# First cross attention: maxima taken from the SBUF copy of the scores, with turns and values a cycle later

## The chip, the core and the metric

The kernel runs on one core of a Trainium2 chip. The metric is device time in microseconds (us) of one execution, lower is better. Engines are called PE or TensorE (matmul), PEld (its weight load), DVE or VectorE, ACT or ScalarE, POOL or GpSimd, and SP (a queue that issues transfers).

## What is computed

The program is a stack of four layers of attention and feed-forward sections over x (16 x 64 x 256, float32) and a context of 16 x 1601 x 256. The change touches its first section, a cross attention with 16 heads of 16, in which the mask is made of scores that are exactly zero at or below the diagonal:

```python
def _L0_xattn_ref(q, k, v, w_q, w_k, w_v, w_o):
    qp, kp, vp = (_split_head(z) for z in (q @ w_q, k @ w_k, v @ w_v))
    scores = jnp.einsum('bhqd,bhkd->bhqk', qp, kp) / jnp.sqrt(jnp.float32(d_k))
    mask = (scores == PAD) & tril
    scores = jnp.where(mask, neg, scores)
    attn = jax.nn.softmax(scores, axis=-1)
    attn = jnp.where(mask, PAD, attn)
    out = jnp.einsum('bhqk,bhkd->bhqd', attn, vp)
    return concat @ w_o
...
x = x + _L0_xattn_ref(_layernorm(x), ctx_1024, ctx_1024, L0_xattn_w_q, ...)
```

## The kernel before, in words

`l0_xattn` (L223 to L530) works on 32 *units*: a batch element and one half of its heads (8 heads, called g). Keys lie on the partitions, 13 *chunks* of 128 to a unit (the last has 65 real keys). A chunk's scores are four matrices of 128 keys x (two heads x 64 queries), one for each row group r of TensorE. Four chunks make a *tile* of 128 x 2048 float32; it fills four PSUM banks, and there is one such buffer (`sc`, tag w, L343). As 13 is not a multiple of 4, a unit takes 3.25 cycles and most units begin within a tile: over a *round* of 13 cycles the units end in cycles 3, 6, 9 and 12.

The main loop (L492 to L525) does one tile per cycle, q = 0 to 103, and everything in it is kept in program order on each engine (`Written`, `mm`, `tr`; these helpers record ScalarE, VectorE and GpSimd operations at L59 and matmuls at L2739 and L2757). A cycle of before issues, in this order:

- for a unit whose maxima were spread in the cycle before: ScalarE copies `mx` to SBUF (L495)
- `take` (ScalarE copies a finished unit's sums) and, for the tile of four cycles ago, `lower` (L402): GpSimd subtracts `mx` from `raw` in SBUF, one operation for each unit in the tile
- `scores(q)` on TensorE
- exp on ScalarE for tile q - 5
- `hide` (L355), where a unit begins: two VectorE operations on the first chunk in PSUM
- ScalarE copies the tile to SBUF (`raw`, L512; seven buffers from two pools)
- `maxima` (L366): per chunk one VectorE operation, top = max(top, scores in PSUM). In the trace these start when ScalarE's copy of the same tile has ended
- two *pieces* of projection of keys and values for later cycles (L334), into PSUM tag `bk` of two buffers; key pieces are copied out by ScalarE, value pieces by VectorE (`keep_values`), `last_keys` by both. A piece may also start the next context load on SP's queue and a small GpSimd operation (`load`, L269)
- `finish` (four small VectorE operations and a matmul group) between the two pieces, for a unit whose values are complete
- `turn_maxima` (L384) in the cycle where a unit ends: TensorE turns `top` into `mt` (tag `bk`), VectorE reduces it to `m`
- near the end, `out(t)`: output projection of a finished block
- `values(q - 5)` on TensorE, with weights from `v` and the exps as moving data, into `acc`
- `spread_maxima` (L394): TensorE spreads `m` over the partitions into `mx` (tag `bk`)

The constant LAG (5) is the number of cycles between a tile's scores and its values; LEAD (4) sets how far the pieces run ahead. GpSimd's subtraction can begin only when `mx` of its unit is in SBUF.

Of the kernel before, what the change touches and what calls it, by code (L numbers as in the profile page):

```python
# [12 lines left out]
F32 = mybir.dt.float32  # L13
I32 = mybir.dt.int32
BF16 = mybir.dt.bfloat16
AF = mybir.ActivationFunctionType
ALU = mybir.AluOpType
AX = mybir.AxisListType
PSUM = bass.MemoryType.PSUM

P = 128
B, S, D = 16, 64, 256
# [3 lines left out]
SK = 1601  # L26
NCH = 13
# [37 lines left out]
class Sections:  # L65
# [57 lines left out]
    def copy(self, out, in_):  # L123

        self.flip ^= 1
        if self.flip:
            self.nc.vector.tensor_copy(out, in_)
        else:
            self.nc.scalar.copy(out, in_)
# [93 lines left out]
    def l0_xattn(self):  # L223
# [6 lines left out]
        with ExitStack() as ctx:  # L230
            sb = ctx.enter_context(tc.tile_pool(name="l0x", bufs=1, reuse_waits="tile"))
            sb2 = ctx.enter_context(tc.tile_pool(name="l0x2", bufs=2, reuse_waits="tile"))
            ps = ctx.enter_context(tc.tile_pool(name="l0x_ps", bufs=2, space=PSUM, reuse_waits="tile"))
            V, A, G = (Written(tc, e) for e in (nc.vector, nc.scalar, nc.gpsimd))
# [15 lines left out]
            pm = ps.tile([P, 512], F32, tag="acc", name="awake")  # L250
# [8 lines left out]
                [sb2.tile([32, 2, 4 * D], F32, tag="raw", name="bias_raw", bufs=4)[:, i] for i in range(2)],  # L259
                sb2.tile([32, 4 * D], BF16, tag="kT", name="part", bufs=5))  # L260

            UNITS, LAG, LEAD = 2 * B, 5, 4
            Q = UNITS * NCH // 4
            xs, us, raws = {}, {}, {}

# [12 lines left out]
                    own.unsqueeze(1).unsqueeze(3).to_broadcast([P, 2, 2, S]), ALU.mult,  # L278
                )

            def keys(b, g, j):
                x = xs[b]
                pm = ps.tile([P, 512], F32, tag="bk", name="pk")
                for k in range(KC):
                    self.columns(
                        pm, wk[:, k, g * P : (g + 1) * P], x.cT[:, k, 512 * j : 512 * j + 512],
                        start=(k == 0), stop=(k == KC - 1))
                x.kT[g, j] = sb2.tile([P, 512], F32, tag="kT", name="kT", bufs=5)
                A.copy(x.kT[g, j], pm)

            def project_values(x, pm, cs):
                for j, c in enumerate(cs):
                    for k in range(KC):
                        self.columns(
                            pm[:, j * D : (j + 1) * D], x.cT[:, k, c * P : (c + 1) * P], wv[:, k, :],
                            start=(j == 0 and k == 0), stop=(k == KC - 1), skip_group_check=True)

            def keep_values(x, pm, cs):
                V.tensor_copy(
                    x.v[:, cs[0] : cs[0] + len(cs), :, :, :16],  # L300
                    pm[:, : len(cs) * D].rearrange("p (j a h e) -> p j a h e", h=2, e=16, a=H // 2))

            def last_keys(b):
                x = xs[b]
                pm = ps.tile([P, 512], F32, tag="bk", name="pk")
                project_values(x, pm, [NCH - 1])
                for g in range(2):
                    for k in range(KC):
                        self.columns(
                            pm[:, (2 + g) * P : (3 + g) * P], wk[:, k, g * P : (g + 1) * P], x.cT[:, k, 1536:1664],  # L310
                            start=False, stop=(k == KC - 1), skip_group_check=True)
                x.last = sb2.tile([P, 2, P], F32, tag="kl", name="kl")
                A.copy(x.last, pm[:, 256:].rearrange("p (g n) -> p g n", g=2))
                keep_values(x, pm, [NCH - 1])

            def two_values(b, i):
                x = xs[b]
                pm = ps.tile([P, 512], F32, tag="bk", name="pk")
                project_values(x, pm, [2 * i, 2 * i + 1])
                keep_values(x, pm, [2 * i, 2 * i + 1])  # L320

            order = [(keys, 0, 0), "v", (keys, 0, 1), "v", (keys, 0, 2), (last_keys,), "v", (keys, 1, 0), "v",
                     (keys, 1, 1), "v", (keys, 1, 2), "v"]
# [7 lines left out]
                    elif b < B:  # L331
                        pieces.append((p[0], b, *p[1:]))

            def piece(i):  # L334
                if 0 <= i < len(pieces) and pieces[i]:
                    f, *args = pieces[i]
                    f(*args)
                if i % NCH == 4 and 0 < i // NCH + 1 < B:
                    load(i // NCH + 1)

# [14 lines left out]
            def hide(q, pm):  # L355

                for i in range(4):
                    if (4 * q + i) % NCH == 0:
                        shape = [S, 4, P]
                        of = pm[:S, :, i, :]  # L360
                        z = sb2.tile(shape, BF16, tag="z", name="z")
                        V.scalar_tensor_tensor(
                            z, of, 0.0, upto[:S].unsqueeze(1).to_broadcast(shape), ALU.is_equal, ALU.mult)
                        V.scalar_tensor_tensor(of, z, NEVER, of, ALU.mult, ALU.add)

            def maxima(q, pm):  # L366

                for i in range(4):
                    n = 4 * q + i
                    u, c = divmod(n, NCH)  # L370
                    if c == 0:
                        us[u] = Streamed(u)
                        us[u].top = sb2.tile([P, 4, P], F32, tag="top", name="top")
                        V.tensor_copy(us[u].top, pm[:, :, i, :])
                        continue
                    w = min(P, SK - c * P)
                    top = us[u].top[:w]
                    V.tensor_tensor(top, top, pm[:w, :, i, :], ALU.max)

            def ends(q):  # L380

                return [n // NCH for n in range(4 * q, 4 * q + 4) if n % NCH == NCH - 1 and 0 <= n < 4 * Q]

            def turn_maxima(u):  # L384

                pt = ps.tile([P, 4, P], F32, tag="bk", name="mt")
                for r in range(4):
                    for j in range(4):
                        o = slice(32 * j, 32 * j + 32)
                        self.mm(pt[o, r, :], us[u].top[:, r, o], self.ident, start=(r == 0), stop=True, skip_group_check=True)  # L390
                us[u].m = sb2.tile([P, 4], F32, tag="m", name="m")
                V.tensor_reduce(us[u].m, pt, AX.X, ALU.max)

            def spread_maxima(u):  # L394

                pt = ps.tile([P, 4, P], F32, tag="bk", name="mx")
                for r in range(4):
                    self.tr(pt[:, r, :], us[u].m[:, r : r + 1].to_broadcast([P, P]), self.ident)
                us[u].mx = sb2.tile([P, 4, P], F32, tag="mx", name="mx", bufs=3)
                us[u].pt = pt  # L400

            def lower(q, E):  # L402

                n, end = 4 * q, 4 * q + 4
                while n < end:
                    u = n // NCH
                    to = min(end, (u + 1) * NCH)
                    part = raws[q][:, :, n - 4 * q : to - 4 * q, :]
                    E.tensor_tensor(part, part, us[u].mx.unsqueeze(2).to_broadcast([P, 4, to - n, P]), ALU.subtract)
                    n = to  # L410

            def values(q):
                e = raws.pop(q)
# [15 lines left out]
            def take(u):  # L429
                us[u].sums = sb2.tile([P, P], F32, tag="sums", name="sums")  # L430
                A.copy(us[u].sums, us[u].acc[:, :P])
# [58 lines left out]
            load(0)  # L490
            self.pinned = True
            for q in range(-(LEAD // 2), Q + LAG):  # L492
                new, old = 0 <= q < Q, 0 <= q - LAG < Q
                for u in ends(q - 1):
                    A.copy(us[u].mx, us[u].pt)  # L495
                closed = ends(q - 1 - LAG)
                for u in closed:
                    take(u)
                if 0 <= q - LAG + 1 < Q:
                    lower(q - LAG + 1, G if q < Q else V)  # L500
                if new:
                    pm = scores(q)
                if old:
                    A.activation(raws[q - LAG], raws[q - LAG], AF.Exp, scale=0.25)
                if new:
                    hide(q, pm)
                    if q % 7 < 3:
                        raws[q] = self.wp.tile([P, 4, 512], F32, tag="w8", name="raw", bufs=3)
                    else:
                        raws[q] = sb2.tile([P, 4, 512], F32, tag="raw", name="raw", bufs=4)  # L510
                    raws[q] = raws[q].rearrange("p r (i n) -> p r i n", n=P)
                    A.copy(raws[q], pm)  # L512
                    maxima(q, pm)
                piece(2 * q + LEAD)
                for u in closed:
                    finish(u)
                piece(2 * q + LEAD + 1)
                for u in ends(q):
                    turn_maxima(u)
                if 0 <= q - Q + 7 < NT - 1:  # L520
                    out(q - Q + 7)
                if old:
                    values(q - LAG)
                for u in ends(q):
                    spread_maxima(u)  # L525
            take(UNITS - 1)
            finish(UNITS - 1)
            self.awake(ps, 3, "bk")
# [2607 lines left out]
```

## Time and profile before

| | us |
|---|---|
| median of 3 runs | 3712.38 (3708.04 to 3714.02) |
| the profiled execution | 3715.3 |
| its span, first to last instruction | 3713.5 |
| TensorE busy in the span | 3370.3 (91%) |
| VectorE / ScalarE / GpSimd busy | 2103.7 / 1608.6 / 1315.9 |
| stretch of the changed loop, 26 to 846 us: TensorE busy | 664.3 of 820 |
| the same stretch: VectorE / ScalarE / GpSimd busy | 458.7 / 454.7 / 467.3 |
| mean granted clock of TensorE in the stretch | 0.97 |

A line of the groups reads: source line, engine, operation, output<-inputs with shapes, number; busy time and mean ns of one; idle time of the engine just before them and what ended most of it. A line of the timeline reads: start, duration, engine, line, operation, output<-inputs, number merged, and in brackets the idle time before it and its releaser. A line of the waits reads: who waited on whom, us in total, times, longest.

### The profile page before, as it was taken

The page shows a single profiled execution, that of the slowest core. Times are in us where ns is not written, and L with a number is a line of the kernel's source. Part 1 is how long each engine was busy: PE and PEld are TensorE (multiplying, and loading weights), DVE is VectorE, ACT ScalarE, POOL GpSimd, SP SyncE. Part 2 cuts the span into 40 slices and gives each one's busy share as a digit, 9 for nine tenths or more (in the row PEclk, how much of TensorE's full clock was granted, in tenths as well). Part 3 has the DMA queues.
Part 4 walks back from the last instruction along what each step waited for, and adds up shares of the span by engine and source line. Part 5 has one row for each costly group of instructions (what it writes and reads, how often), then busy time and mean ns, then how long its engine had stood idle before and what let it go on. Part 6 is the DMA issues. An engine that isn't in the chain of part 4 may idle for free.

```text
span 3713.5 us, 93831 instructions
## 1 busy us (share of the span) xinstructions
PE 3370.3 (91%) x42270; PEld 2086.1 (56%) x42270; DVE 2103.7 (57%) x4048; ACT 1608.6 (43%) x2149; POOL 1315.9 (35%) x721
## 2 busy tenths in 40 slices
PE   7888888787999989999997998999999889999997
PEld 4555555554556664555555666565656555555454
DVE  5555555555555545665656545577777765333445
ACT  3555555543444423444433434366666612111123
POOL 3566566640111013333332100477787630000002
PEclk9999999988999989999998999999999999999998
DMA  3100111101223345432201000311111004111550
GB/s 121 40 31 29 39 40 40 40 5 67 93 87 103 115 140 188 148 129 74 94 26 41 1 6 9 105 40 58 39 58 40 9 4 176 39 39 33 244 213 13
DMA packets 108305, 261.42 MB, mean 70 GB/s; under 512 B 9625, under 2 KB 76316, under 8 KB 105600
## 3 DMA queue, kind: packets, MB, share of 16 engines
q1 hardware_dynamic: 99184, 223.34, 17.0%
q10 hardware_dynamic: 6912, 27.27, 2.3%
q8 instruction: 332, 5.44, 0.6%
q0 software_dynamic: 1808, 4.80, 0.4%
q14 instruction: 69, 0.57, 0.0%
HBM read 249.05 MB, written 6.33 MB: 69 GB/s over the span
## 4 chain that ended last, share of the span: by engine, by line
PE 65%; DVE 21%; ACT 9%; issue 4%; POOL 0%; DMA 0%; another core or an unknown queue 0%; SPq 0%; ACTq 0%; DVEq 0%; POOLq 0%
PE pk L2739 11%; PE sc L2739 10%; DVE top L59 7%; PE lin L2739 7%; ACT raw L59 5%; PE lin_t L2739 5%; PE pu L2739 4%; PE acc L2739 3%; PE gate L2286 3%; PE up L2286 3%; PE lin L216 3%; PE pc L1906 3%; PE prz L2739 2%; PE turn L2757 2%; PE gelu_t L1820 2%
## 5 line engine op out<-in xcount | busy, mean ns | idle before, releaser
L59 POOL TENSOR_TENSOR raw<-raw,mx 128x2048 f32<-128x2048 f32 (+3 forms) x123 | 460.0, 3772 | 342.4 <-ACT mx L59 342.4
L2668 POOL TENSOR_TENSOR tot<-tot,e 128x1024 f32<-128x1024 f32 (+1 forms) x170 | 405.7, 2387 | 105.8 <-ACT e L2052 78.9
L59 DVE TENSOR_TENSOR top<-top,sc 128x512 f32<-128x512 f32 (+1 forms) x384 | 263.8, 687 | 314.8 <-ACT raw L59 304.9
L2739 PE MATMUL sc<-qb,kT 32*128 32x128 f32 x6400 | 244.1, 286 | 81.1 <-DVE top L59 63.5
L2049 DVE SCALAR_TENSOR_TENSOR e<-sc,row_L_xattn_nbias,free 128x2048 f32<-128x2048 f32 x104 | 244.3, 2349 | 105.7 <-PE sc L2739 102.8
L2051 ACT ACTIVATE e<-e 128x2048 f32<-128x2048 f32 x104 | 198.7, 1910 | 231.7 <-DVE e L2049 231.7
L2739 PEld LDWEIGHTS sc<-qb,kT 32*128 32x128 f32 x6400 | 205.1, 189 | 120.4 <-ACT raw L59 40.8
L59 ACT COPY raw<-sc 128x2048 f32<-128x2048 f32 x104 | 193.8, 1864 | 116.6 <-PE sc L2739 62.1
L2739 PE MATMUL pk<-wv,cT 128*32 128x256 f32 x3328 | 212.0, 394 | 0.1
L2739 PE MATMUL pk<-cT,wk 128*32 128x512 f32 (+1 forms) x2048 | 202.1, 516 | 0.0
L2052 ACT ACTIVATE e<-e 128x2048 f32<-128x2048 f32 x104 | 198.8, 1912 | 3.3
L59 ACT ACTIVATE raw<-raw 128x2048 f32<-128x2048 f32 x104 | 199.3, 1918 | 1.7 <-POOL raw L59 0.9
L2739 PE MATMUL pk<-wkv,cT 128*32 128x256 f32 x3328 | 193.5, 381 | 0.0
L2739 PE MATMUL pk<-cT,wkv 128*32 128x512 f32 (+1 forms) x2048 | 192.5, 514 | 0.0
L2290 ACT ACTIVATE g<-gate 128x512 f32<-128x512 f32 x68 | 40.6, 597 | 293.6 <-PE gate L2286 293.6
L1906 PE MATMUL pc<-ew,eh 128*128 128x256 f32 x640 | 156.1, 386 | 0.0
L2739 PEld LDWEIGHTS pk<-wv,cT 128*32 128x32 f32 x3328 | 104.8, 113 | 83.2 <-issue 27.7
L2291 DVE TENSOR_TENSOR hT<-up,g 128x512 f32<-128x512 f32 x68 | 47.0, 692 | 183.9 <-PE up L2286 183.9
L1439 POOL TENSOR_TENSOR e<-e,mx 128x512 f32<-128x512 f32 x96 | 81.9, 885 | 193.7 <-DVE mx L1438 193.7
L2739 PE MATMUL sc<-cT,qT 128*64 128x512 f32 (+1 forms) x768 | 142.1, 520 | 4.7 <-ACT scs L1419 4.2
L2327 POOL TENSOR_TENSOR x<-x,row_L_xattn_bv 128x1024 f32<-128x1024 f32 x2 | 4.7, 2347 | 398.2 <-DVE xln L158 398.2
L2739 PE MATMUL pu<-cn,e 128*64 128x257 f32 (+1 forms) x1248 | 141.2, 381 | 2.0 <-POOL e L1449 2.0
(550 smaller groups left out, 6847.2 us busy)
## 6 DMA issues: line engine op xcount, KB each, us to landing
cT<-in_ctx_t SPq DMA_DIRECT2D x128, 832.0 KB
cn<-in_ctx_n SPq DMA_DIRECT2D x32, 1664.0 KB
piece<-in_ctx_n ACTq DMA_DIRECT2D x32, 640.0 KB
w<-in_L_attn_W SPq DMA_DIRECT2D x8, 1024.0 KB
piece<-in_ctx_n ACTq DMA_DIRECT2D x16, 384.0 KB
w<-in_L_ffn_W SPq DMA_DIRECT2D x16, 256.0 KB
down<-in_L_ffn_w_down SPq DMA_DIRECT2D x16, 256.0 KB
gate<-in_L_ffn_w_gate SPq DMA_DIRECT2D x16, 256.0 KB
```

Source lines behind the costliest of these rows:

```text
L59: ins = getattr(self.engine, name)(*args, **kw)
L216: nc.tensor.matmul(pm, xT[:, k, t * P : (t + 1) * P], w[:, k, :], start=(k == 0), stop=(k == kc - 1))
L1439: pin(nc.gpsimd.tensor_tensor(p.e, p.e, p.mx.unsqueeze(2).to_broadcast(p.shape), ALU.subtract))
L1820: nc.tensor.matmul(pm, w[:, c, lo : lo + m], cT[:, c, :], start=(c == 0), stop=(c == nk - 1))
L1906: nc.tensor.matmul(pc[:, n, j, :], s.eh[i][:, c, tok], ew2[:, c, cols], start=False, stop=(c == 3))
L2049: nc.vector.scalar_tensor_tensor(e16, pm16, nb, free[:, at : at + P].unsqueeze(1).to_broadcast([P, 16, P]), ALU.add, ALU.mult)
L2051: nc.scalar.activation(e, e, AF.Relu)
L2052: nc.scalar.activation(e, e, AF.Square)
L2286: nc.tensor.matmul(pm[-1], w[:, k, n * P : (n + 1) * P], xT[:, k, tok], start=(k == 0), stop=(k == KC - 1))
L2668: nc.gpsimd.tensor_tensor(tot[:w], x.first if c == 1 else tot[:w], e[:w], ALU.add)
L2739: ins = self.nc.tensor.matmul(*args, **kw)
L2757: ins = self.nc.tensor.transpose(*args)
```

## The change

- ScalarE alone reads the scores from PSUM. VectorE takes the maxima from `raw` in SBUF. Where a tile holds several whole chunks of a unit, one `tensor_reduce` over the chunks (elements 128 floats apart) gives their maximum, straight into `top` if it is the unit's first part, else into a tile `some` that a `tensor_tensor` folds into `top`. One chunk alone is folded or copied directly. A unit's last chunk (65 rows) is always folded by itself.
- `maxima` is issued after the first piece instead of ahead of it.
- In each cycle the first piece, of whatever kind, is copied out by ScalarE and the second by VectorE.
- `turn_maxima` is issued one cycle later, behind the next tile's scores; `spread_maxima` and the copy of `mx` one cycle later too.
- LAG is 6. Exp is issued at the end of a cycle, for the tile whose values come in the next.
- `lower` works for one more cycle on GpSimd at the end (q = 104), and shares the new helper `parts`.

```diff
-            UNITS, LAG, LEAD = 2 * B, 5, 4
+            UNITS, LAG, LEAD = 2 * B, 6, 4
...
-            def keys(b, g, j):
+            def keys(copy, b, g, j):
...
-                A.copy(x.kT[g, j], pm)
+                copy(x.kT[g, j], pm)
...
-            def piece(i):
+            def piece(i, copy):
                 if 0 <= i < len(pieces) and pieces[i]:
                     f, *args = pieces[i]
-                    f(*args)
+                    f(copy, *args)
...
-            def maxima(q, pm):
-
-                for i in range(4):
-                    n = 4 * q + i
-                    u, c = divmod(n, NCH)
+            def maxima(q):
+
+                raw = raws[q]
+                for u, lo, hi in parts(q):
+                    c = 4 * q + lo - u * NCH
+                    last = c + hi - lo == NCH
+                    n = hi - lo - last
                     if c == 0:
                         us[u] = Streamed(u)
                         us[u].top = sb2.tile([P, 4, P], F32, tag="top", name="top")
-                        V.tensor_copy(us[u].top, pm[:, :, i, :])
-                        continue
-                    w = min(P, SK - c * P)
-                    top = us[u].top[:w]
-                    V.tensor_tensor(top, top, pm[:w, :, i, :], ALU.max)
+                    top = us[u].top
+                    to = top
+                    if n and c:
+                        to = sb2.tile([P, 4, P], F32, tag="some", name="some", bufs=1)
+                    if n == 1 and c == 0:
+                        V.tensor_copy(top, raw[:, :, lo, :])
+                    elif n == 1:
+                        V.tensor_tensor(top, top, raw[:, :, lo, :], ALU.max)
+                    elif n:
+                        V.tensor_reduce(to, raw[:, :, lo : lo + n, :].rearrange("p r i n -> p r n i"), AX.X, ALU.max)
+                        if c:
+                            V.tensor_tensor(top, top, to, ALU.max)
+                    if last:
+                        w = SK - (NCH - 1) * P
+                        V.tensor_tensor(top[:w], top[:w], raw[:w, :, hi - 1, :], ALU.max)
+
+            def parts(q):
+
+                n, end = 4 * q, 4 * q + 4
+                while n < end:
+                    to = min(end, (n // NCH + 1) * NCH)
+                    yield n // NCH, n - 4 * q, to - 4 * q
+                    n = to
...
-                new, old = 0 <= q < Q, 0 <= q - LAG < Q
-                for u in ends(q - 1):
+                new, old, low = 0 <= q < Q, 0 <= q - LAG < Q, 0 <= q - LAG + 1 < Q
+                for u in ends(q - 2):
                     A.copy(us[u].mx, us[u].pt)
...
-                if 0 <= q - LAG + 1 < Q:
-                    lower(q - LAG + 1, G if q < Q else V)
+                if low:
+                    lower(q - LAG + 1, G if q <= Q else V)
                 if new:
                     pm = scores(q)
-                if old:
-                    A.activation(raws[q - LAG], raws[q - LAG], AF.Exp, scale=0.25)
+                for u in ends(q - 1):
+                    turn_maxima(u)
                 if new:
                     hide(q, pm)
...
                     A.copy(raws[q], pm)
-                    maxima(q, pm)
-                piece(2 * q + LEAD)
+                piece(2 * q + LEAD, A.copy)
+                if new:
+                    maxima(q)
                 for u in closed:
                     finish(u)
-                piece(2 * q + LEAD + 1)
-                for u in ends(q):
-                    turn_maxima(u)
+                piece(2 * q + LEAD + 1, V.tensor_copy)
...
                 if old:
                     values(q - LAG)
-                for u in ends(q):
+                for u in ends(q - 1):
                     spread_maxima(u)
+                if low:
+                    A.activation(raws[q - LAG + 1], raws[q - LAG + 1], AF.Exp, scale=0.25)
```

More of the change, by code (lines that the diff above doesn't have):

```diff
@@ L296, in project_values, with keep_values, last_keys @@
                             start=(j == 0 and k == 0), stop=(k == KC - 1), skip_group_check=True)
-            def keep_values(x, pm, cs):
-                V.tensor_copy(
+            def keep_values(copy, x, pm, cs):
+                copy(
                     x.v[:, cs[0] : cs[0] + len(cs), :, :, :16],
                     pm[:, : len(cs) * D].rearrange("p (j a h e) -> p j a h e", h=2, e=16, a=H // 2))
-            def last_keys(b):
+            def last_keys(copy, b):
                 x = xs[b]
@@ L312, in last_keys, with two_values @@
                 x.last = sb2.tile([P, 2, P], F32, tag="kl", name="kl")
-                A.copy(x.last, pm[:, 256:].rearrange("p (g n) -> p g n", g=2))
-                keep_values(x, pm, [NCH - 1])
-            def two_values(b, i):
+                copy(x.last, pm[:, 256:].rearrange("p (g n) -> p g n", g=2))
+                keep_values(copy, x, pm, [NCH - 1])
+            def two_values(copy, b, i):
                 x = xs[b]
@@ L319, in two_values @@
                 project_values(x, pm, [2 * i, 2 * i + 1])
-                keep_values(x, pm, [2 * i, 2 * i + 1])
+                keep_values(copy, x, pm, [2 * i, 2 * i + 1])
             order = [(keys, 0, 0), "v", (keys, 0, 1), "v", (keys, 0, 2), (last_keys,), "v", (keys, 1, 0), "v",
@@ L402, in lower @@
             def lower(q, E):
[L404 to L410, printed above, removed]
+                for u, lo, hi in parts(q):
+                    part = raws[q][:, :, lo:hi, :]
+                    E.tensor_tensor(part, part, us[u].mx.unsqueeze(2).to_broadcast([P, 4, hi - lo, P]), ALU.subtract)
             def values(q):
```

## The prediction

> **What bounds the kernel now.** I read the page's groups first, then the waits of the stretch 26 to 846 us, in which the changed loop runs its 104 cycles, then one cycle in order of time. In the groups I look at who waits on whom over a score tile:
>
> ```profile
> L59 POOL TENSOR_TENSOR raw<-raw,mx 128x2048 f32<-128x2048 f32 (+3 forms) x123 | 460.0, 3772 | 342.4 <-ACT mx L59 342.4
> L59 DVE TENSOR_TENSOR top<-top,sc 128x512 f32<-128x512 f32 (+1 forms) x384 | 263.8, 687 | 314.8 <-ACT raw L59 304.9
> L59 ACT COPY raw<-sc 128x2048 f32<-128x2048 f32 x104 | 193.8, 1864 | 116.6 <-PE sc L2739 62.1
> ```
>
> VectorE's maxima follow ScalarE's copy of the same tile, one after the other. The waits of the stretch (us in total, times, longest) show what TensorE pays for that:
>
> ```profile
> PE sc L2739 <- DVE top L59: 68.9, 60, 4.1
> PE mt L2739 <- DVE top L59: 46.6, 30, 1.9
> PE mx L2757 <- DVE m L59: 24.7, 29, 2.0
> ```
>
> In the windows view TensorE is busy 664.3 of these 820 us; 140 of the missing 155.7 us are these three waits. One cycle in order of time:
>
> ```profile
> 414.87 1.17 PE L2739 MATMUL sc<-qb,kT 32*128 32x128 f32 x32 [1.64 <-DVE top L59]
> 415.98 1.92 PE L2739 MATMUL pk<-cT,wk 128*32 128x512 f32 x16
> 416.16 1.87 ACT L59 COPY raw<-sc 128x2048 f32<-128x2048 f32 x1 [2.02 <-PE sc L2739]
> 417.72 1.91 PE L2739 MATMUL pk<-wv,cT 128*32 128x256 f32 x32
> 418.06 2.85 DVE L59 TENSOR_TENSOR top<-top,sc 128x512 f32<-128x512 f32 x4 [2.73 <-ACT raw L59]
> 419.44 1.08 PE L2739 MATMUL acc<-raw,v 128*32 128x64 f32 x64
> ```
>
> Scores 1.17, copy 1.87 and maxima 2.85 us in series, with gaps, make the 6.2 us to the next scores (421.06); TensorE's own steps take 1.11 + 1.74 + 1.72 + 1.08 = 5.65. I count in rounds of 13 cycles (4 units), after which the pattern repeats: 8 rounds in 817 us (first scores 25.9, last 842.8) are 102.1 us each. TensorE's floor for a round is 13 x 5.65 + 4 x 1.95 (mt 1.08, mx 0.65, the sums about 0.2) = 81.3.
>
> **The change, part by part.**
>
> *The score tile is free after the copy.* The next scores no longer wait for 2.85 us of maxima. Were nothing else late, the round would fall from 102.1 towards 81.3, so at most 8 x 20.8 = 166 us are to be had.
>
> *The maxima themselves.* A round has 52 DVE operations of 0.69 (35.9 us). They become 9 reductions of 2048 elements, 2 of 1536 and 2 of 1024, plus 15 two-input maxima and a copy. The nearest rows for a reduction are 2287 ns (L588, 2048) and 1215 ns (L2872, 1024), so the reductions take about 26 us; DVE's own 128x512 rows with both inputs in SBUF take 692 ns, so the rest is 11 us. VectorE's round stays at about 59.6 us (hide 4 x 1.4, finish 4 x 1.4, values 13 x 0.68, m 4 x 0.68 beside it). This edit saves VectorE nothing.
>
> *A new collision.* Before, a maximum read one operand from PSUM. Now 15 a round have both in SBUF, beside GpSimd's subtraction of 4.6 us that reads SBUF too. What that does is seen elsewhere in this trace:
>
> ```profile
> 2162.78 2.00 POOL L1918 TENSOR_TENSOR vn<-xi,row_L_ffn_router_b 128x1024 f32<-128x1024 f32 x1 [34.48 <-DVE v L1931]
> 2163.22 2.65 DVE L1922 SCALAR_TENSOR_TENSOR a<-a,v 128x1024 f32<-128x1024 f32 x1
> ...
> 2099.48 1.22 DVE L1919 TENSOR_TENSOR sp<-sp,rb 128x1024 f32<-128x1024 f32 x1
> 2099.64 2.91 POOL L1918 TENSOR_TENSOR vn<-xi,row_L_ffn_router_b 128x1024 f32<-128x1024 f32 x1 [23.35 <-DVE v L1931]
> ```
>
> The VectorE operation, 1.22 us by itself, took 2.65: it ended 1.1 us after GpSimd's did. The other way round GpSimd's 2.00 became 2.91. [...] L457 at 822.04 shows who wins at a boundary: VectorE's second operation (2620 ns against 485) ended 0.5 us after the first of three GpSimd subtractions, so it got in between.
>
> *Laying the cycles out*, with these durations and each engine's order. GpSimd works off four cycles' scores per unit (15.1 us) as soon as mx is copied. Take the cycle that copies mx as zero. Subtractions end at 5.45, about 10.75 and 16.05. VectorE's first maximum (scores 1.3, copy 1.9, reduction 2.25) is ready at 5.45 and gets in. The next cycle hides (hide until 8.35, copy until 10.3), its first maximum gets in at 10.75; the unit's last one, right behind, waits for 16.05. So `top` is there at 16.75, where TensorE wanted to turn it at 12.6: 4.1 us lost. Then VectorE does a reduction 1.2, finish 1.4 and the value copy 0.7 until 20.0, and only that frees the `bk` buffer of the next projection: 2.1 us more. Then projection, projection, values and mx (1.75 + 1.75 + 1.05 + 0.65) end at 25.3, and mx starts the next GpSimd run. The next two units, laid out alike, take 24.7 and 24.6, and the last, of four cycles, 31.0: 105.6 a round. If the very first maximum just misses its boundary, 107. Before, it was 102.1. The score wait is gone, but the chain mx, GpSimd 15.1 with two or three maxima of 0.7 let in, last maximum, turn, projections, mx is as long. That is 3.5 to 5 us a round, 28 to 40 in all; I take 30, nearer to the layout that I could follow.
>
> *The reduction's stride.* It reads elements 512 bytes apart, which no VectorE row of before does. [...] The nearest row with such steps is ScalarE's `kept<-pb`, 64-byte steps from PSUM: 259 ns for 128 elements, against 266 for `sums<-acc` without steps. [...] A gain below 2.2 is excluded: contiguous rows show no faster.
>
> *Turn, mx, exp and values later.* The turn moves from the end of a cycle to behind the next scores. It is a wait on TensorE in front of two projections, which the layout counts. The mx copy, with GpSimd behind it, comes a cycle later, and LAG 6 moves its users by the same. Exp now stands at a cycle's end and waits for the subtraction of the same cycle (done about 5.5 to 6.2 us into it when a unit's first tile is full), with the next score copy queued behind it on ScalarE: 0.5 us once a round, hidden where the next cycle hides first (it does there). The raw buffers (7) are just enough for LAG 6, because the old reader stands before the new scores on TensorE itself. The tail has one cycle more; its chain from the last scores is the old one: 0 to 3 us. If the cover fails, exp costs up to 2 us a unit, 64 in all.
>
> *First piece on ScalarE, second on VectorE.* A copy takes 0.59 on the one and 0.68 on the other, and each engine had one a cycle before; `last_keys` puts two on one engine (0.4 us, 16 times). Hidden, as ScalarE has 455 busy us in the 820; if not, 6 us. A value copy on ScalarE writes runs of 16, as VectorE's did; I put it at 0.59 and at 0.68 at worst. Context loads keep their place on SP's and GpSimd's queues.
>
> Sum: the profiled execution took 3715.3 us (1.8 more than its span), so 3745; the median of before is 2.9 lower, which gives 3742.
>
> **The rivals.**
>
> *The collisions rarely bite* (0.28). GpSimd is idle some 30 us of a round, and a maximum that comes at a boundary pays nothing. With no lock wait the same layout gives 88 a round (buffer stalls of 1.75, 0.7, 0.9, 0.4 and small gaps on 84), or 3600. Against it: three of the four units have a second maximum directly behind the first. With half of the waits gone it is 95 a round: 3655, faster.
>
> *The stride costs* (0.24). [...]
>
> *The two effects cancel.* Between layout and rival lies no change (0.08).
>
> **How the numbers follow.** Locks as laid out, 0.40 (3720 to 3790): slower. With the stride that is slower 0.64, faster 0.28, same 0.08. Within 0.2% is 7.4 us, about what a measurement of this kernel can tell. The range goes from three quarters of the full gain without lock waits (3712 - 0.77 x 112 = 3625) to the stride case with some lock waits more (3850).
>
> **What would show it.** TensorE's wait for `top` before scores gone, and a wait for `top` before mt grown from 46.6 to over 80 us. The two-input maxima in SBUF at a mean of 2 us or more, with minimum near 0.69 and maximum near 5. Reductions of 2048 near 2.3 us. New waits of pk on the value copy. GpSimd's subtractions longer by up to 0.7. If the maxima stay at 0.7 us, or the turn never waits, the forecast is wrong and the kernel is faster; if the reduction takes over 4 us, it is far slower.

## The result and the profile after

The kernel after takes 3737.2 us (median of 4 runs, 3732.7 to 3750.8), the one before, measured beside it, 3713.2: a ratio of 1.0072, 95% interval 1.0043 to 1.0101. It is slower, by 24 us; the forecast was 3742. The profiled execution of after took 3750.8 us, the slowest of its four, so its spans are a little long. The experiments below were measured in three groups, each with its own runs of before (medians 3712.4, 3713.7 and 3709.2); ratios are to the before of the same group.

First the groups of the page of after that answer to those of before (the helper is still L59, the matmuls are at L2756 now):

```profile
L59 POOL TENSOR_TENSOR raw<-raw,mx 128x2048 f32<-128x2048 f32 (+3 forms) x123 | 473.6, 3881 | 379.8 <-ACT mx L59 249.8
L59 DVE TENSOR_REDUCE some<-raw 128x512 f32<-128x2048 f32 (+1 forms) x80 | 275.2, 3439 | 81.3 <-ACT raw L59 81.2
L59 ACT COPY raw<-sc 128x2048 f32<-128x2048 f32 x104 | 194.4, 1870 | 208.2 <-DVE sc L59 150.9
L59 DVE TENSOR_TENSOR top<-top,some 128x512 f32<-128x512 f32 x80 | 157.7, 1971 | 2.7
```

An operation of 0.69 us takes 1.97 on average, with almost no idle time ahead of it: the wait lies within the time recorded for it. The reduction over four chunks is in a row of mixed shapes. Taken by shape and tile (for a tile: minimum, median and maximum in ns, then when):

```profile
L59 DVE TENSOR_REDUCE some<-raw 128x512 f32<-128x2048 f32 x64 | 249.8, 3904 | 63.6 <-ACT raw L59 63.5
L59 DVE TENSOR_TENSOR top<-top,some x80: 671/1088/9596, 40.2 to 899.4; 128x512 f32<-128x512 f32 x80
```

It takes 3.90 us, where I assumed 2.29. Three chunks take 1.92 and two 1.24, not far from contiguous data (1.74 and 1.22 in the run with contiguous groups below). TensorE's waits in 26 to 846 us:

```profile
PE pk L2756 <- DVE kT L59: 71.5, 32, 7.2
PE pk L2756 <- DVE v L59: 39.8, 23, 8.8
PE mt L2756 <- DVE top L59: 38.1, 19, 3.1
PE sc L2756 <- ACT raw L59: 6.2, 10, 1.3
```

The wait of the scores for `top` is gone, as meant. In its place the projections wait for VectorE's copies out of `bk`, 111 us in all. How one of these comes about is seen in the order of time:

```profile
431.53 11.51 POOL L59 TENSOR_TENSOR raw<-raw,mx 128x1024 f32<-128x1024 f32 x3 [10.02 <-DVE xT L59]
...
437.95 9.58 DVE L59 TENSOR_TENSOR top<-top,some 128x512 f32<-128x512 f32 x1
...
442.99 0.62 POOL L59 TENSOR_TENSOR qb<-qT,cst 128x256 f32<-128x256 f32 x1
443.56 3.42 POOL L59 TENSOR_TENSOR raw<-raw,mx 128x1536 f32<-128x1536 f32 x1
447.45 0.68 DVE L59 COPY v<-pk 128x512 f32<-128x512 f32 x1
...
448.19 3.64 PE L2756 MATMUL pk<-wv,cT 128*32 128x256 f32 x32 [8.57 <-DVE v L59]
```

The fold begins at 437.95, while GpSimd subtracts, and ends at 447.53, 0.55 us after GpSimd's last operation (446.98). It did not get in at 438.5 (where the second of the three subtractions in the first row gives way to the third), nor at 442.99, nor at 443.56. All the waits in the trace of after have this pattern. Of the 120 two-input maxima, 64 took over 0.15 us more than 0.69, and each of these ended 0.55 us (0.01 more or less) after the end of a GpSimd operation; of the 56 others four began in the last 0.03 to 0.05 us of a GpSimd operation and none of the rest while GpSimd ran. 60 of the 64 got in when the first operation ended that was running as they began. Four were passed over at one boundary or at three, and took 8.5 and 9.6 us. Behind the fold shown here stands the value copy, and behind that TensorE for 8.57 us. And TensorE comes back slower: the same projection took 1.94 us at 427.42 and takes 3.64 now. The windows view (PE busy is the first column with a count, the granted clock the number behind the last count) shows the reason:

```profile
430.00:438.00 8.00, 7.82 (x203) 5.12 (x195) 5.96 (x8) 4.97 (x5) 6.47 (x2) 1.00 0.01 2
438.00:448.00 10.00, 1.62 (x16) 0.26 (x8) 10.00 (x2) 4.08 (x3) 8.98 (x4) 0.77 0.01 2
448.00:452.00 4.00, 3.81 (x48) 1.99 (x52) 3.44 (x5) 0.00 (x0) 0.00 (x0) 0.50 0.00 0
452.00:456.00 4.00, 4.00 (x129) 3.41 (x123) 0.77 (x2) 0.27 (x1) 0.00 (x0) 0.78 0.79 270
```

The clock falls within the gap, at about 443.5, 3.9 us after TensorE's last matmul ended. In windows of half a microsecond it is 0.50 until 453.5, 0.77 in the next and 1.00 from 454.0 on, some 5.5 us after TensorE came back.

### The profile page after: what moved, and what is told of

Read it like the earlier page. It is cut to its first block, busy times and chain, and to the rows that moved or that the text cites. A ratio compares the mean times of both kernels' runs of the same rounds, so it can differ in the third digit from the quotient of the medians.

```text
span 3749.0 us, 93657 instructions
## 1 busy us (share of the span) xinstructions
PE 3387.2 (90%) x42270; PEld 2093.3 (56%) x42270; DVE 2360.1 (63%) x3863; ACT 1610.5 (43%) x2150; POOL 1334.1 (36%) x721
## 4 chain that ended last, share of the span: by engine, by line
PE 65%; DVE 24%; ACT 6%; issue 2%; DMA 1%; POOL 0%; SPq 0%; ACTq 0%; DVEq 0%; POOLq 0%
PE pk L2756 13%; PE sc L2756 9%; PE lin L2756 6%; DVE top L59 6%; PE lin_t L2756 5%; DVE some L59 4%; PE acc L2756 4%; PE pu L2756 4%; ACT raw L59 3%; PE gate L2303 3%; PE up L2303 3%; PE lin L216 3%; PE pc L1923 3%; PE prz L2756 2%; PE gelu_t L1837 2%
## 5 line engine op out<-in xcount | busy, mean ns | idle before, releaser
L59 POOL TENSOR_TENSOR raw<-raw,mx 128x2048 f32<-128x2048 f32 (+3 forms) x123 | 473.6, 3881 | 379.8 <-ACT mx L59 249.8
L59 DVE TENSOR_REDUCE some<-raw 128x512 f32<-128x2048 f32 (+1 forms) x80 | 275.2, 3439 | 81.3 <-ACT raw L59 81.2
L59 ACT COPY raw<-sc 128x2048 f32<-128x2048 f32 x104 | 194.4, 1870 | 208.2 <-DVE sc L59 150.9
L2756 PE MATMUL pk<-cT,wk 128*32 128x512 f32 (+1 forms) x2048 | 228.7, 575 | 60.9 <-DVE kT L59 47.3
L2756 PE MATMUL pk<-wv,cT 128*32 128x256 f32 x3328 | 212.7, 396 | 57.8 <-DVE v L59 28.4
L2756 PE MATMUL sc<-qb,kT 32*128 32x128 f32 x6400 | 241.6, 285 | 24.1 <-DVE e L2066 17.9
L2756 PEld LDWEIGHTS sc<-qb,kT 32*128 32x128 f32 x6400 | 201.4, 188 | 62.6 <-DVE e L2066 22.2
L59 ACT ACTIVATE raw<-raw 128x2048 f32<-128x2048 f32 x104 | 199.6, 1919 | 24.7 <-POOL raw L59 20.4
L2756 PE MATMUL pk<-wkv,cT 128*32 128x256 f32 x3328 | 193.5, 381 | 0.0
L2756 PE MATMUL pk<-cT,wkv 128*32 128x512 f32 (+1 forms) x2048 | 192.5, 514 | 0.0
L2756 PEld LDWEIGHTS pk<-wv,cT 128*32 128x32 f32 x3328 | 105.5, 114 | 147.0 <-DVE v L59 40.3
L59 DVE TENSOR_TENSOR top<-top,some 128x512 f32<-128x512 f32 x80 | 157.7, 1971 | 2.7
L2756 PEld LDWEIGHTS pk<-cT,wk 128*32 128x32 f32 x2048 | 66.2, 120 | 148.4 <-issue 70.9
```

Source lines behind the costliest of these rows:

```text
L59: ins = getattr(self.engine, name)(*args, **kw)
L2756: ins = self.nc.tensor.matmul(*args, **kw)
```

## The experiments

The theories: L, VectorE's two-input maxima in SBUF wait for GpSimd; S, the four-chunk reduction costs more than contiguous data; M, the moves (turn, exp, pieces) cost the time. All runs keep the rest of the program.

**Contiguous groups.** The reduction takes neighbouring elements; the maxima are then those of the wrong groups.

```diff
-  V.tensor_reduce(to, raw[:, :, lo : lo + n, :].rearrange("p r i n -> p r n i"), AX.X, ALU.max)
+  V.tensor_reduce(to, raw[:, :, lo : lo + n, :].rearrange("p r i n -> p r (i n)").rearrange("p r (m k) -> p r m k", k=n), AX.X, ALU.max)
```

> The kernel after, with one change: each reduction takes its groups of neighbouring elements instead of elements 512 bytes apart; same sizes and counts, but the maxima are of the wrong groups. What theory S (the stride of the four-chunk reductions, 3.9 us where 2.3 was assumed, 72 of them, 116 us of VectorE's time) expects: reductions of 2048 at 2.3 us, and the kernel at 3690 us or less, faster than before. Theory L (VectorE's two-input maxima wait for GpSimd's subtractions, 119 us in the trace of after): the waits stay, the two-input maxima at 1.9 us still, and the kernel at 3720 to 3740. Theory M (the later turn, later exp and the pieces' copies, not the maxima): 3725 to 3745.

**No two-input maximum.** Each fold becomes a one-input reduction; the running maximum is left out.

```diff
-  V.tensor_tensor(top, top, to, ALU.max)
+  V.tensor_reduce(top, to.unsqueeze(3), AX.X, ALU.max)
```

(and likewise the two other `tensor_tensor` of `maxima`)

> The kernel after, with every two-input maximum in SBUF turned into a one-input reduction that only copies: the fold of the running maximum is left out, the number of operations stays. Theory L: no VectorE operation waits for GpSimd any more, operations of 512 elements at 0.6 to 0.7 us, 119 us of VectorE's waiting gone, and the kernel at 3620 to 3680. Theory S: the four-chunk reductions stay at 3.9 us, and the kernel stays over 3715. Theory M: 3725 to 3745.

**Both edits.**

> Both edits at once (contiguous groups, no two-input maximum; the maxima are wrong in both ways). This is the case without locks and without a stride penalty, which the layout of the prediction put at 88 us a round: 3600. Theories L and S both expect 3590 to 3650, and that this gain is shared between the two single edits as their theory says; theory M expects that less than 30 us come back: 3705 or more.

**Maxima from PSUM, all else as in after.** `maxima(q, pm)` is the old function, called where the new one stands, behind the first piece.

```diff
-                    maxima(q)
+                    maxima(q, pm)
```

> The kernel after with its whole schedule (turn, mx, exp and values later, pieces split between the engines), but with the maxima taken from the scores in PSUM, four operations of 0.69 us a tile, as before. Neither a lock nor a stride is left, but the score tile is again free only after the maxima. Theories L and S: the schedule itself is harmless, so 3695 to 3720. Theory M: the schedule is what costs, so 3735 or more.

Measured (the last four side by side with before on one chip, after with another before):

| | us | ratio to before (95%) |
|---|---|---|
| after | 3737.2 | 1.0072 (1.0043 to 1.0101) |
| contiguous groups | 3694.8 | 0.9953 (0.9938 to 0.9968) |
| no two-input maximum | 3643.3 | 0.9817 (0.9798 to 0.9837) |
| both | 3569.8 | 0.9616 (0.9596 to 0.9637) |
| maxima from PSUM | 3630.7 | 0.9788 (0.9768 to 0.9809) |

That the edits took away what they were meant to is seen by shape, first for contiguous groups, then for no two-input maximum:

```profile
L59 DVE TENSOR_TENSOR top<-top,some 128x512 f32<-128x512 f32 x80 | 177.0, 2213 | 2.7
L59 DVE TENSOR_REDUCE some<-raw 128x512 f32<-128x2048 f32 x64 | 146.0, 2281 | 92.8 <-ACT raw L59 92.8
```

```profile
L59 DVE TENSOR_REDUCE some<-raw 128x512 f32<-128x2048 f32 x64 | 250.1, 3908 | 74.2 <-ACT raw L59 74.0
L59 DVE TENSOR_REDUCE top<-some 128x512 f32<-128x512 f32 x80 | 54.9, 686 | 2.7
```

The waits are not wholly gone in the run with no two-input maximum. A unit's first chunk, where it stands alone, is copied inside SBUF, and these copies waited now, which in after they had not (413 to 417 ns):

```profile
L59 DVE COPY top<-raw x8: 413/1567/1626, 91.4 to 754.5; 128x512 f32<-128x512 f32 x8
```

Each late one ended 0.28 to 0.29 us after the end of a GpSimd operation. That is 8 us of waiting in this run and 9 in the run with both edits, so the cost of the waits is put a little low below.

So L and S both hold, but not with every number expected: contiguous groups came out 5 us above what S had put, both edits 20 us below the least that L and S had put. On this chip after would stand at 3712.4 x 1.0072 = 3739. Taking away the waits for GpSimd (the locks of the prediction) brings 96 us, the stride 44, both 169. Each alone, put upon the run with neither, costs 125 (waits) and 73 (stride). M falls: the moved steps with the old maxima are 82 us *faster* than before, which no theory had expected. The run with neither cost is another 61 us below that; as VectorE's busy time differs little between the two (483.3 and 465.7 us of the loop, in the table further down), this is about what the earlier release of the score tile would be worth.

**Which of the moves helps.** The pieces are copied as before (keys by ScalarE, values by VectorE), on top of maxima from PSUM.

```diff
-                copy(x.kT[g, j], pm)
+                A.copy(x.kT[g, j], pm)
```

(`last_keys` and `keep_values` likewise)

> As the run with the maxima from PSUM and the rest of the schedule of after, but with key pieces copied by ScalarE and value pieces by VectorE as before. That run was 82 us faster than before. If the later turn and spreading give this (TensorE's waits for top before mt, 46.6 us, and for m before mx, 24.7 us, fell to 3.0 and 1.0), 3625 to 3650. If the split of the copies gives it, 3690 or more.

3654.6 us, 0.9845 (0.9829 to 0.9860), 5 us above the range put for the later turn and spreading: most of the gain is kept without the split, and the split adds 21 to 28 us by the ratios (0.9788 and, in a second measurement further down, 0.9770). It shows in TensorE's waits before the scores, 102.3 us here against 76.8 with the split:

```profile
PE sc L2744 <- DVE top L59: 80.9, 80, 4.1
PE sc L2744 <- ACT raw L59: 21.4, 13, 1.7
```

What is left of the gain, 59 us, belongs to the moves of this schedule together: turn and spreading, but also LAG 6, the place of exp and the maxima behind the first piece, which no run took back one by one. That it is turn and spreading is read from the waits alone. The waits of the kernel with the maxima from PSUM, 26 to 846 us, show only one of the three of before left:

```profile
PE sc L2744 <- DVE top L59: 76.3, 74, 4.1
...
DVE m L59 <- PE mt L2744: 39.3, 30, 3.1
```

TensorE's waits of mt for `top` (46.6 before) and of mx for `m` (24.7) have become VectorE's wait for the turn. The first is 3.0 in this stretch, the second no longer there: 68 us of waiting gone.

**Small reductions.** Computes the same as after: four chunks by two reductions over two, into slots of a tile that also holds the running maximum, and one reduction over the slots.

```diff
-  V.tensor_reduce(to, raw[:, :, lo : lo + n, :].rearrange("p r i n -> p r n i"), AX.X, ALU.max)
-  if c:
-      V.tensor_tensor(top, top, to, ALU.max)
...
+  ms = [2, 2] if n == 4 else [n]
...
+  for m, k in zip(ms, slots):
+      V.tensor_reduce(fold[:, k], raw[:, :, lo : lo + m, :].rearrange("p r i n -> p r n i"), AX.X, ALU.max)
+      lo += m
...
+      V.tensor_reduce(to, fold[:, first:end].rearrange("p k r n -> p r n k"), AX.X, ALU.max)
```

> The kernel after, computing the same, with the reductions cut small: four chunks as two reductions over two chunks (1.24 us each in the trace of after) into slots of a tile that also holds the running maximum, and one reduction over the three slots (1.9) as the fold. 5 two-input maxima a round are left of 15, and no reduction over four. If locks and stride together are the cause, most of both losses is gone: between the run without either (3570) and the one that keeps the maxima in PSUM (3631), 3580 to 3625. If only the count of VectorE's operations and their sum matter (about 51 us a round for the maxima, as in after without its waits), 3640 to 3660, as in the run that had only the locks taken away.

**The last five replaced too**: two copies into slots and a reduction over two (one copy where the last whole chunk stands alone, as the running maximum is in a slot already).

```diff
-  V.tensor_tensor(top[:w], top[:w], raw[:w, :, hi - 1, :], ALU.max)
+  V.tensor_copy(fold[:w, 1], top[:w])
+  V.tensor_copy(fold[:w, 2], raw[:w, :, hi - 1, :])
+  V.tensor_reduce(top[:w], fold[:w, 1:3].rearrange("p k r n -> p r n k"), AX.X, ALU.max)
```

> As the run with small reductions, and the last 5 two-input maxima of a round replaced too: two one-input copies into slots and a reduction over two (about 2 us where it was 0.69 plus its wait). If a wait for GpSimd costs more than 1.4 us on average at these five places (6.3 us was the mean wait of the long ones), this is faster than the run with small reductions, by up to 30 us; if VectorE's sum decides, it is slower by 8 x 5 x 1.4 = 56 us at most.

Measured 3688.0 (0.9927, 0.9912 to 0.9942) and 3744.1 (1.0080, 1.0061 to 1.0100). The first misses both of its expectations, the second is at the far end of its own. By tile, the small reductions first, then the run with the last five replaced:

```profile
L59 DVE TENSOR_TENSOR top<-top,raw x32: 686/992/2162, 51.3 to 836.0; 65x512 f32<-65x512 f32 x32
L59 DVE TENSOR_TENSOR top<-fold,raw x8: 3523/4095/4142, 70.0 to 767.8; 128x512 f32<-128x512 f32 x8
```

```profile
L59 DVE COPY fold<-raw x48: 409/417/3840, 50.1 to 890.7; 65x512 f32<-65x512 f32 x32, 128x512 f32<-128x512 f32 x16
L59 DVE COPY fold<-top x32: 410/470/4526, 48.0 to 890.3; 65x512 f32<-65x512 f32 x32
```

The few two-input maxima that were left still wait (the eight of the second line took 3.5 us or more each), and they all stand at a unit's end, right ahead of the turn. TensorE's wait of mt for `top` in the loop was 14.2 us in the run with no two-input maximum; in these two it is:

```profile
PE mt L2771 <- DVE top L59: 63.7, 21, 4.8
```

```profile
PE mt L2775 <- DVE top L59: 111.0, 31, 6.1
```

In the second run the copies, which have one input, take up to 3.8 and 4.5 us instead of 0.41: with SBUF copies in place of the maxima the long operations are still there.

VectorE's sum is not what made the first run miss. Less the waits inside its maxima, 45.5 us, VectorE is busy 571 us of the loop, against 590 in the run with no two-input maximum, which by the ratios was 41 us faster. The waits themselves and their place are what is left. The second run waits as long in all (48 us), and VectorE has 53 us more of work, all of it right ahead of the turn; that is near the 56 us between the two. Whether the sum or the place of that work counts was not separated.

**What makes the reduction slow**, by itself: 48 more reductions behind the end of the small-reduction kernel, at distances of 512, 528, 544 and 576 bytes.

```diff
+  for gap in (128, 132, 136, 144):
+      for n in (2, 3, 4):
+          at = wide.rearrange("p r i n -> p (r i n)")[:, : 16 * gap].rearrange("p (r i n) -> p r i n", r=4, i=4)
+          for _ in range(4):
+              nc.vector.tensor_reduce(got, at[:, :, :n, :P].rearrange("p r i n -> p r n i"), AX.X, ALU.max)
```

> The run with small reductions, with 48 more reductions on VectorE behind the end of the program: 512 results from 2, 3 or 4 elements each, which lie 512, 528, 544 or 576 bytes apart, four times each, with nothing beside them. If the distance of 512 bytes collides with itself, only the four-element form at 512 takes 3.9 us and the others 2.3. If four lines at a time are too many at any distance, all four-element forms take 3.9. If GpSimd and ScalarE beside it made it slow in after, it takes 2.3 here at every distance.

```profile
L3168 DVE TENSOR_REDUCE got<-wide 128x512 f32<-128x2048 f32 x16 | 57.9, 3618 | 0.6
L3168 DVE TENSOR_REDUCE got<-wide 128x512 f32<-128x1536 f32 x16 | 30.5, 1909 | 0.6
L3168 DVE TENSOR_REDUCE got<-wide 128x512 f32<-128x1024 f32 x16 | 19.7, 1231 | 0.6
```

Four elements to a result cost 3.62 us, at each distance (taken apart by time: 3.618 at 512 bytes, 3.630 at 528, 3.610 at 544, 3.617 at 576). Three cost 1.91 and two 1.23; contiguous groups of the same sizes took 2.28, 1.74 and 1.22. So here it is the number of elements taken from far apart, not their distance between 512 and 576 bytes, and not the engines beside it, which add 0.3 us at most (3.90 in after).

**Crossing the readers.** Maxima from PSUM again; ScalarE copies two banks of the tile while VectorE takes the maxima of the other two.

```diff
-                    A.copy(raws[q], pm)
+                    A.copy(raws[q][:, :2], pm[:, :2])
+                    maxima(q, pm, 1)
+                    A.copy(raws[q][:, 2:], pm[:, 2:])
...
+                    maxima(q, pm, 0)
```

> As the run with the maxima from PSUM and the schedule of after (3631), but ScalarE copies the banks 0 and 1 of the score tile while VectorE takes the maxima of banks 2 and 3, and then the other way round: 2 copies of 1024 and 8 maxima of 256 a tile. Computes the same. If each engine waits only for the banks that it shares with the other, the tile is free about 3.4 us after its scores instead of 4.8 (copies about 1.0 each, four maxima of about 0.42 each = 1.7), and most of the last wait of TensorE (sc for top, 76 us in 820) goes: 3570 to 3610. If a reader of any part of the tile waits for the other engine's reader of any other part, the four steps follow one another in 5.4 us and the kernel is slower than 3631: 3660 to 3700.

> The run with the maxima from PSUM and the schedule of after once more, on the chip of the run by halves, to compare the two: 3625 to 3640, 0.976 to 0.981 of before.

3730.4 (1.0059, 1.0043 to 1.0074) against 3624.5 (0.9770, 0.9756 to 0.9783) on one chip. The steps follow one another, so it is slower, and by 106 us, more than the 30 to 70 that I had put for this case:

```profile
416.21 1.01 ACT L59 COPY raw<-sc 128x1024 f32<-128x1024 f32 x1 [2.41 <-DVE sc L59]
417.25 1.33 DVE L59 TENSOR_TENSOR top<-top,sc 128x256 f32<-128x256 f32 x3 [1.16 <-ACT raw L59]
...
418.50 0.41 DVE L59 COPY top<-sc 128x256 f32<-128x256 f32 x1
418.95 1.01 ACT L59 COPY raw<-sc 128x1024 f32<-128x1024 f32 x1 [1.73 <-DVE top L59]
419.99 1.33 DVE L59 TENSOR_TENSOR top<-top,sc 128x256 f32<-128x256 f32 x3 [1.08 <-ACT raw L59]
```

In this program a reader of the tile waited for the reader ahead of it, on other banks too: in these rows VectorE 1.16 and 1.08 us for ScalarE's copy, and ScalarE 1.73 us for VectorE. The best version found is therefore the schedule of after with the maxima of before: 2.1 to 2.3% faster than before.

## Why the prediction was right, and where it was not

The table sums up the loop (first to last scores) in the profiled execution of each (that of contiguous groups, 3711.9, was its slowest); us, by the windows view. "Idle" is the loop less TensorE's busy time. "A round" is the loop divided by 8, as in the prediction; but from the first scores to the last there are 103 cycles, not 104, so that a true round is 1% longer in every row.

| | loop | a round | VectorE busy | TensorE busy | TensorE idle | clock |
|---|---|---|---|---|---|---|
| before | 817.6 | 102.2 | 458.8 | 663.5 | 154.1 | 0.97 |
| after | 868.7 | 108.6 | 708.1 | 694.2 | 174.5 | 0.93 |
| contiguous groups | 812.8 | 101.6 | 612.4 | 685.5 | 127.3 | 0.93 |
| no two-input maximum | 758.6 | 94.8 | 597.7 | 670.8 | 87.8 | 0.96 |
| both | 690.1 | 86.3 | 483.3 | 643.8 | 46.3 | 0.99 |
| maxima from PSUM | 740.1 | 92.5 | 465.7 | 649.7 | 90.4 | 0.98 |

The sign and the number came out, but not by the sum that I wrote, so that the number is luck. 3742 was the waits for GpSimd without a stride penalty. That case was built (contiguous groups): 3695, *faster* than before. Two errors, 47 us too much for one and 44 for a cost left out, met.

*The loop and the whole.* I had 28 to 40 us for the loop and 0 to 3 for its tail. In the profiled executions the loop grew by 51 and the span by 35.5, as all that follows the last scores took 15.6 us less; 3 of these are the stage's own tail. The rest of the program behind the stage, which no version changes, took 2841.6 us in the profile of before, 2828.8 in that of after and up to 2847.8 in the others. Differences of some 15 us between two profiles are therefore not the change's.

*The round of before.* 102.1 divides the 817 us of 103 cycles by 8; 13 of these cycles take 103.1. Against this the layout's 105.6 to 107 was only 2.5 to 4 longer, 20 to 31 us in all and not 28 to 40.

*The score tile is free after the copy.* Right as a bound of 166 us: with neither cost 142.6 are gained, and the loop is 127.5 shorter. But I booked all of it under the tile: 82 of the 142 come without any earlier release, by the moved steps and the split pieces, and 61 with the release. I listed mt's 46.6 and mx's 24.7 and never asked what the moved turn alone does to them.

*VectorE's work is 59.6 a round.* 60.4 in the run with neither (483.3 / 8). Right. The layout without waits for GpSimd gave 88 a round; measured 86.3.

*The collision.* Right in kind. The waits inside the maxima of after are 80 x (1.97 - 0.69) for the folds and 17 us for the 40 others, 119 us or 14.9 a round. Where the step failed is its price for the round: 105.6 to 107 laid out, 101.6 measured. The waits add 15.3 to the round without them; I had 17.6 to 19, on a floor that was 1.7 too high. My rule that VectorE gets in at the first boundary between GpSimd's operations held for 60 of the 64 maxima that waited. The four others, of which the one at 437.95 is shown, waited 33 us together, and longer each (up to 8.9 us) than any that I had laid out; what decides at a boundary stays open. Still the sum is smaller, as half of the folds (the median is 1.09 us) lose no more than 0.4.

*Who pays.* I expected mt to wait for `top` for over 80 us and measured 38.1, less than before. I did name the value copy and its `bk` buffer as the next in line, for 2.1 us a unit. VectorE's copies out of `bk` are the main payer, 111 us, and nearly two thirds of it are key copies, which the change had moved to VectorE and which I had put at nothing. With the split taken back in the run with the maxima from PSUM the time rises by 21 to 28, so the split is a gain there. Whether it is a cost in after, where VectorE is held up, no run shows: the split was not taken back alone in after.

*The stride.* Wrong. I took ScalarE's row, from PSUM with 64-byte steps, for VectorE in SBUF with 512. With two elements from far apart nothing shows (1.24 us against 1.22 contiguous), with three a tenth (1.92 against 1.74), with four the reduction takes 3.6 to 3.9 us instead of 2.28. The reason for the step from three to four was not shown. VectorE's rounds grow by 14.3 (597.7 against 483.3 over 8).

*The rival in which the stride costs* had both costs, and the range ends at 3850 with it, 113 us above what was measured. It stood on 24.5 us a round more for the reductions, an estimate of mine that no run shows, and on 20 for the waits; the runs showed 14.3 and 14.9. VectorE was busy for 88.5 of a round of 108.6. With 160.6 us of the loop free on VectorE, part of the two costs overlaps: 169 us together, 198 if each alone is added.

*Exp, buffers, tail.* From the last scores to the end of the stage 28.4 us before, 25.4 after: no cost, as said. *GpSimd's subtractions* of 2048 went from 4.59 to 4.70, within the 0.7 named.

*Not in the prediction at all:* the clock. Of the 51 us that the loop grew, 20 are TensorE's idle time and 31 its longer busy time for the same matmuls (694.2 against 663.5), at a granted clock of 0.93 instead of 0.97 (663.5 x 0.97 / 0.93 would be 692). In the gap of 8.6 us shown above it fell from 1.00 to 0.50 after 3.9 us of idle time, and was back at 1.00 some 5.5 us after the next matmul began. I counted each stall once; behind this one a projection took 3.64 us instead of 1.94 as well.

## What to carry to other kernels

Price a moved operand by where its inputs lie: two inputs in SBUF on VectorE, beside a GpSimd stream, cost more here (96 to 125 us) than the early release of the tile was worth (about 61). When a change has several parts, lay out each of them alone; here the better kernel was the change without its main idea. For a reduction over far-apart elements measure the exact count of elements to a result, as three and four differed by a factor of 1.9 here (1.91 and 3.62 us).

## What the runs showed of the hardware

- A VectorE reduction in SBUF to 512 results from elements that lie far apart, with nothing beside it: 1.23 us for two elements each, 1.91 for three, 3.62 for four (3.61 to 3.63 at distances of 512 to 576 bytes).
- In after, 64 VectorE maxima with two inputs in SBUF began while GpSimd worked and took 0.98 to 9.60 us instead of 0.69, each ending 0.55 us after the end of a GpSimd operation, 60 of them after the one that ran as they began. Four were passed over and took 8.5 to 9.6 us; one took 11.3 in the run with contiguous groups. One-input reductions of the same size took 677 to 689 ns, all 80 of them, in the run with no two-input maximum. One-input float32 copies inside SBUF, 0.41 us alone, took up to 4.5 in the run with the last five replaced. The unit's first copy took 413 to 417 ns in after, where none began while GpSimd ran, and in the run with no two-input maximum 1.6 us in seven of eight places.
- In a gap of 8.6 us on TensorE the granted clock fell to 0.50 after 3.9 us, and it was back at 1.00 some 5.5 us after the gap.
